# Four heads' maxima first, four heads' exponentials second: regrouping the score runs of an attention slot

## The chip, the cores and the metric

The kernel runs on one core of a Trainium2 chip. The metric is the device time of one execution in microseconds. The core has five instruction streams: TensorE (PE, whose weight loads the profile lists apart as PEld), VectorE (DVE), ScalarE (ACT), GpSimd (POOL) and SyncE (SP, which here only issues DMAs). Each works through its own queue in order, and they wait for each other through semaphores.

## The reference

One transformer layer on x of shape (2, 1024, 512), all in float32: a layer norm, attention with 32 heads of 16 features, a residual, a second layer norm, a quantised gated feed-forward part (512 to 1376 to 512), and a second residual. Cut to what matters here:

```python
q, k, v = (proj(w_q), proj(w_k), proj(w_v))          # (B, 32, S, 16)
scores = jnp.einsum('bhqd,bhkd->bhqk', q, k) / jnp.sqrt(jnp.float32(D_K))
attn = jax.nn.softmax(scores, axis=-1)
out = jnp.einsum('bhqk,bhkd->bhqd', attn, v)
x = x + out.transpose(0, 2, 1, 3).reshape(B, S, HIDDEN) @ w_o.T
x = x + ffn(layernorm(x))      # int4 inputs, ternary weights, relu squared, int8 middle
```

With 2 batches, 32 heads and 1024 by 1024 scores, the attention scores are by far the largest thing computed, and they are computed twice: once for the maximum of each row of scores, once for the exponentials.

## The kernel before, in words

**Steps and slots.** The attention is cut into 32 steps (`steps`): 2 batches, 2 blocks of 512 queries, 4 groups of eight heads, 2 halves of a group. A step thus holds four heads, 512 queries and all 1024 keys. Each step has eight slots (`NT`) of work of two kinds:

- A maximum slot takes four heads and 128 queries by 512 keys (`max_mm`, line 590). Queries stand on the PSUM partitions, so VectorE reduces along the row (`max_reduce`, line 600). After eight such slots all row maxima of the step are there; `max_parts` and `max_rows` turn them into a row `mrow` by four small TensorE transposes into a tile `psn` (line 613).
- An exponential slot takes four heads, 128 keys and 512 queries (`exp_mm`, line 630). Keys stand on the partitions. Three matmuls add up: two for the product of k with the two parts (high and low) of q, and one that adds minus the maximum (`mrow` with `onesr`). ScalarE takes the exponential (`exponentials`, line 634).

Then `weigh_values` (line 660) multiplies the exponentials with v, four heads side by side in the columns of the array, and adds up over the eight slots of the step in one PSUM bank (`pso`).

**Row groups.** A head with its two parts takes 32 rows of TensorE's array of 128, so the four heads of a step lie on four row groups, r = 0 to 3. A tile of scores holds two heads: the pair j = 0 is r = 0 and 1, the pair j = 1 is r = 2 and 3. A tile is 128 partitions by 1024 float32, two PSUM banks. The pool `ps_s` has three such tiles (`bufs=3`), handed out in turn by `scores_psum`, for `psm` (maxima), `pse` (exponentials) and, once in a step, `psn`. Two further banks hold `pso` (pool `ps_a`) and one tile `o` for all filler work (pool `ps_o`).

**The order of work.** The order of instructions is written out by hand: each engine executes them in the order in which the Python code issues them. The loop over T (line 1400) is a software pipeline: slot T issues the maxima of slot T (step `nm`, place `im`), the exponentials of slot T - 10 (`LE`; step `ne`, place `ie`) and the product with v of slot T - 11 (step `nw`, place `iw`). In each slot there are two runs of scores, and `scores(exps, maxs)` issues one run: it takes the tiles from the pool, issues the matmuls of all its tiles in turns (`l` = 0, 1, 2), then the readers of its tiles, the exponentials ahead of the maxima.

In the mixed slots, which are nearly all, the first run takes the exponentials of the pair 0 and the maxima of the pair 1; then comes the product with v, short filler work, the second run with the exponentials of the pair 1 and the maxima of the pair 0, and then the longer filler work. The opening ten slots have only maxima, the last ten only exponentials; these come as one run of four heads.

**Fillers.** All other work (projections of q, k and v, layer norms, the output projection, the feed-forward part of finished rows, the quantising of weights) is cut into small generators. The class `Fillers` hands them out by a planner: `fill.run` gives out work until an estimated cost is used up, and counts its own runs for gaps; neither looks at measured time. A filler that needs TensorE takes the bank `o`, and in the mixed slots at most one filler gets it in each run of the planner. The end of the last block of queries (`the_end`) is ordered by a list scheduler of its own.

Of the kernel before, what the change touches and what calls it, by code (L numbers as in the profile page):

```python
# [233 lines left out]
def kernel(  # L234
# [101 lines left out]
    def scores_psum(name):  # L336
        return ps_s.tile([P, 2, QB], F32, tag="s", name=name)
# [224 lines left out]
    def places(n):  # L562
        kst[n] = sb.tile([P, S], F32R, tag="kst", name=f"kst_{n}", bufs=3)
        qst[n] = [sb.tile([P, QB], F32R, tag="qst", name=f"qst_{n}_{l}", bufs=6) for l in range(2)]

    def load_k(n, first=0):
        nc.sync.dma_start(kst[n][:, first:].bitcast(F32), step_k(n)[:, :, first:])

    def load_q(n):
        b, h, g, s = steps[n]  # L570
        for l, q in enumerate(qst[n]):
            rows = qD[b, g, h][l].rearrange("(r s e) q -> s r e q", r=4, s=2)[s]
            nc.sync.dma_start(q.bitcast(F32), rows)

    def load_v(n):
        b, h, g, s = steps[n]
        vt[n] = sb.tile([P, NT, 4, 32], F32, tag="v", name=f"v_{n}", bufs=2)
        nc.sync.dma_start(vt[n].rearrange("p t r e -> p (t r e)"), vD[b, g, s].rearrange("p t e -> p (t e)"))

    def max_tile(n, i, j):  # L580

        if i == 0 and n not in pm:
            pm[n] = sp.tile([P, TQ, 2, 4], F32, tag="pm", name=f"pm_{n}")
        return scores_psum(f"psm_{n}_{i}_{j}")

    def max_mm(n, i, j, ps, l):
        kh, t = divmod(i, TQ)
        for r in (2 * j, 2 * j + 1):
            rows = slice(32 * r, 32 * r + 32)
            nc.tensor.matmul(  # L590
                ps[:, r % 2, :],
                qst[n][l][rows, t * P : (t + 1) * P],
                kst[n][rows, kh * QB : (kh + 1) * QB],
                start=(l == 0),
                stop=(l == 1),
            )

    def max_reduce(n, i, j, ps):
        kh, t = divmod(i, TQ)
        nc.vector.tensor_reduce(pm[n][:, t, kh, 2 * j : 2 * j + 2], ps, AX.X, ALU.max, negate=True)  # L600

    def max_parts(n):
        m = sp.tile([P, TQ, 4], F32, tag="m", name=f"m_{n}")
        p = pm.pop(n)
        nc.vector.tensor_tensor(m, p[:, :, 0, :], p[:, :, 1, :], ALU.min)
        cols = mcols[n % 2].rearrange("p t (r c) -> p t r c", r=4)
        nc.vector.tensor_copy(cols[:, :, :, 0], m)
        nc.vector.tensor_tensor(cols[:, :, :, 1], m, cols[:, :, :, 0].bitcast(F32), ALU.subtract)
# [12 lines left out]
    def exp_mm(n, i, j, ps, l):  # L621
        for r in (2 * j, 2 * j + 1):
            rows = slice(32 * r, 32 * r + 32)
            if l < 2:
                left, right = kst[n][rows, i * P : (i + 1) * P], qst[n][l][rows, :]
            else:

                rows = slice(32 * r, 32 * r + 2)
                left, right = onesr[rows, :], mrow[n][rows, :]
            nc.tensor.matmul(ps[:, r % 2, :], left, right, start=(l == 0), stop=(l == 2))  # L630

    def exponentials(n, i, j, ps):
        e = sb.tile([P, 2, QB], F32, tag="e", name=f"e_{n}_{i}_{j}", bufs=4)
        nc.scalar.activation(e, ps, AF.Exp, scale=SCALE)  # L634
        probs.setdefault((n, i), {})[j] = e

    def scores(exps, maxs):


        es = [(*x, scores_psum(f"pse_{x[0]}_{x[1]}_{x[2]}")) for x in exps]  # L640
        ms = [(*x, max_tile(*x)) for x in maxs]
        for l in range(3):
            for x in es:
                exp_mm(*x, l)
            if l or not es:
                for x in ms:
                    max_mm(*x, l - bool(es)) if l - bool(es) < 2 else None
        for x in es:
            exponentials(*x)
        for x in ms:  # L650
            max_reduce(*x)
# [3 lines left out]
    def weigh_values(n, i):  # L655
        if i == 0:
            acc[n] = ps_a.tile([P, QB], F32, tag="a", name=f"pso_{n}")
        e = probs.pop((n, i))
        for r in range(4):
            nc.tensor.matmul(  # L660
                acc[n][32 * r : 32 * r + 32, :],
                vt[n][:, i, r, :],
                e[r // 2][:, r % 2, :],
                start=(i == 0),
                stop=(i == NT - 1),
            )
        if i == NT - 1:
            po[n] = sb.tile([P, QB], F32, tag="po", name=f"po_{n}", bufs=3)
            nc.scalar.copy(po[n], acc[n])

    def normalise(n):


        b, h, g, _ = steps[n]
        p0, p1 = po.pop(n - 1), po.pop(n)
        dD = dram.tile([4, 2, QB], F32, name=f"dD_{n}")
        rD = dram.tile([4, 2, QB], F32, name=f"rD_{n}")
        yield ("gap", 3)
        for s, p in enumerate((p0, p1)):
            nc.sync.dma_start(dD[:, s, :], p[16 * (1 - s) :: 32, :])  # L680
        yield ("gap", 4)
        k = 8 * QB // P
        den = sp.tile([P, k], F32, tag="den", name=f"den_{n}", bufs=2)
        nc.sync.dma_start(den, bass.AP(dD.tensor, dD.offset, [[k, P], [1, k]]))
        yield ("gap", 6)
        for c in (slice(0, QB // 2), slice(QB // 2, QB)):
            nc.vector.copy_predicated(p0[:, c], second.to_broadcast([P, QB // 2]), p1[:, c])
            yield ("gap", 1)
        nc.vector.reciprocal(den, den)
        yield ("gap", 2)  # L690
        nc.sync.dma_start(bass.AP(rD.tensor, rD.offset, [[k, P], [1, k]]), den)
        yield ("gap", 3)
        rden = sb.tile([P, QB], F32, tag="rden", name=f"rden_{n}", bufs=1)
        nc.sync.dma_start(
            rden, bass.AP(rD.tensor, rD.offset, [[QB, 8], [0, 16], [1, QB]])
        )
        yield ("gap", 4)
        OT[b, h, g] = sb.tile([P, QB], F32, tag="OT", name=f"OT_{b}_{h}_{g}", bufs=5)
        nc.gpsimd.tensor_tensor(OT[b, h, g], p0, rden, ALU.mult)  # L699
# [617 lines left out]
    def load_slot(n):  # L1317

        return NT * n - (4 if n == 2 else 5)
# [5 lines left out]
    def due_v(n):  # L1325
        return NT * n + (8 if n < 8 else 5)
# [64 lines left out]
    def feed():  # L1391

        while ffns and set(ffns[0][2]) <= fill.done | {ffns[0][2][0]}:
            name, gen, after, due, cost, by = ffns.popleft()
            fill.add(name, gen, after, "ffn", due, cost, by)
# [4 lines left out]
    for T in range(LE + NT * NSTEP + 1):  # L1400
        fill.slot = T
        ne, ie = divmod(T - LE, NT)
        nm, im = divmod(T, NT)
        nw, iw = divmod(T - LE - 1, NT)

        fill.scores = int(T < LE - 1 or T >= NT * NSTEP)

        n = T // NT + 1
        if 1 < n < NSTEP and T == load_slot(n):
            b, h, g, s = steps[n]  # L1410
            fill.ensure(f"k_{b}_{g}_0", f"k_{b}_{g}_1", f"q_{b}_{g}_{h}")
            places(n)
            load_k(n)
            load_q(n)
        n = (T - 5) // NT
        if 0 <= n < NSTEP and T == due_v(n):
            b, h, g, s = steps[n]
            fill.ensure(f"v_{b}_{g}_0", f"v_{b}_{g}_1")
            load_v(n)
        if im == 0 and 0 < nm <= NSTEP:  # L1420
            max_parts(nm - 1)
        exps = [(ne, ie, j) for j in range(2)] if 0 <= ne < NSTEP else []
        maxs = [(nm, im, j) for j in (1, 0)] if nm < NSTEP else []
        mixed = bool(exps and maxs)
        if mixed:
            scores(exps[:1], maxs[:1])
        elif exps:
            scores(exps, [])
        if 0 <= nw < NSTEP:
            weigh_values(nw, iw)  # L1430
            if iw == NT - 1 and nw % 2 and nw < NSTEP - 1:
                b, h, g, _ = steps[nw]
                fill.add(f"norm_{b}_{h}_{g}", normalise(nw), (), "back")
            if iw == NT - 1 and nw == NSTEP - 2:
                fill.add("tokens", first_tokens(nw), (), "ffn", 0)
        feed()
        fill.run(100.0, short=True)
        if mixed:
            scores(exps[1:], maxs[1:])
        elif maxs:  # L1440
            scores([], maxs)
        if im == 1 and 0 < nm <= NSTEP:
            max_rows(nm - 1)
        share = min(max(fill.pace([w[4:] for w in ffns]), SHARE), MORE)
        left = fill.run(share + min(left, SHARE))
# [52 lines left out]
```

## Time and profile before

| | |
|---|---|
| time, median of 3 runs | 1178.94 us (1177.97 to 1180.83) |
| profiled execution, span | 1179.7 us |
| TensorE matmuls busy | 1154.8 us, 98% |
| VectorE busy | 868.8 us, 74% |
| ScalarE busy | 686.8 us, 58% |
| GpSimd busy | 264.1 us, 22% |
| granted TensorE clock, mean | 0.999 |
| row maxima (line 600) | 512 of 1222 ns |
| exponentials (line 634) | 512 of 1023 ns |

The span is that of one profiled execution, from its first to its last instruction; it lies within the range of the timed runs. Busy time counts an engine as busy while any of its instructions is running. TensorE's matmuls overlap each other, in different row or column groups of the array and in the pipeline, so their durations can't be added up. The timeline lists instructions in order of time: start, duration, engine, line, operation, what is written and what is read, shapes, how many were merged into one line (x8), and in brackets how long the engine had been idle before and what ended that. For TensorE the starts of the weight loads tell best when a block of work begins.

### The profile page before, as it was taken

The numbers are of one execution on the slowest core, as the hardware profiler recorded it, in microseconds if no ns is written. First come the engines' busy times: TensorE is split into PE (matmuls) and PEld (weight loads), VectorE is DVE, ScalarE is ACT, GpSimd is POOL, SyncE is SP. The second block draws the span as 40 slices with busy tenths as digits, with TensorE's granted clock in tenths as the row PEclk, the third lists the DMA queues.
The fourth block names the chain that finished last, engine by engine and source line by source line (L and its number), as shares of the span: only waits on it lengthen the run. The fifth ranks groups of instructions, "written<-read, shape, count | busy, mean of one in ns | idle before, by whom it ended". The sixth has DMA issues, their size and how long they took to land.

```text
span 1179.7 us, 21990 instructions
## 1 busy us (share of the span) xinstructions
PE 1154.8 (98%) x8922; PEld 522.5 (44%) x8922; DVE 868.8 (74%) x1261; ACT 686.8 (58%) x878; POOL 264.1 (22%) x319
## 2 busy tenths in 40 slices
PE   8899999999999999999999999999999999999998
PEld 5454444544444444544444445444444433444344
DVE  6765577898876677788866665786988788888467
ACT  2058765556565556566665555465666555665746
POOL 3224336465501101221011011022110001220111
PEclk9999999999999999999999999999999999999999
DMA  5666765556623323443633324244442516362300
GB/s 157 174 183 194 249 197 176 172 190 197 194 93 96 103 55 110 113 95 77 94 86 121 124 59 147 84 130 138 84 97 60 89 53 83 58 81 55 79 9 37
DMA packets 97099, 135.35 MB, mean 115 GB/s; under 512 B 34829, under 2 KB 54285, under 8 KB 96997
## 3 DMA queue, kind: packets, MB, share of 16 engines
q1 hardware_dynamic: 87204, 105.75, 34.6%
q0 software_dynamic: 9792, 28.19, 7.7%
q8 instruction: 70, 1.15, 0.4%
q14 instruction: 33, 0.26, 0.1%
HBM read 89.25 MB, written 37.19 MB: 107 GB/s over the span
## 4 chain that ended last, share of the span: by engine, by line
PE 81%; DVE 5%; DMA 5%; issue 2%; POOL 2%; SPq 2%; ACT 2%; POOLq 0%; DVEq 0%; ACTq 0%
PE pse L630 25%; PE pso L660 18%; PE psm L590 9%; PE psv L533 4%; PE psk L476 4%; PE psy L847 4%; PE psq L476 4%; PE pu L937 2%; PE py L1006 2%; DVE pm L600 2%; PE pg L937 2%; DMA rden<-rD 1%; PE psn L613 1%; SPq L505 1%; PE end L1161 1%
## 5 line engine op out<-in xcount | busy, mean ns | idle before, releaser
L600 DVE TENSOR_REDUCE pm<-psm 128x2 f32<-128x1024 f32 x512 | 623.8, 1222 | 242.9 <-PE pse L630 146.0
L634 ACT ACTIVATE e<-pse 128x1024 f32<-128x1024 f32 x512 | 522.7, 1023 | 408.2 <-PE pse L630 307.3
L590 PE MATMUL psm<-kst,qst 32*128 32x512 f32 x2048 | 369.5, 444 | 7.3 <-DMA kst<-kD 3.8
L630 PE MATMUL pse<-qst,kst 32*128 32x512 f32 x2048 | 367.6, 442 | 3.9 <-DVE pm L600 3.1
L630 PEld LDWEIGHTS pse<-qst,kst 32*128 32x128 f32 x2048 | 149.2, 183 | 332.8 <-issue 199.7
L660 PE MATMUL pso<-e,v 128*32 128x512 f32 x2048 | 272.9, 605 | 0.0
L630 PE MATMUL pse<-mrow,onesr 2*128 2x512 f32 x1024 | 203.9, 396 | 0.0
L590 PEld LDWEIGHTS psm<-kst,qst 32*128 32x128 f32 x2048 | 151.3, 183 | 25.5 <-ACT e L634 10.8
L630 PEld LDWEIGHTS pse<-mrow,onesr 2*128 2x128 f32 x1024 | 94.5, 183 | 3.3
L951 POOL TENSOR_TENSOR g<-g 128x460 f32<-128x460 f32 (+1 forms) x36 | 34.7, 964 | 244.7 <-ACT g L947 237.4
L660 PEld LDWEIGHTS pso<-e,v 128*32 128x32 f32 x2048 | 40.4, 108 | 94.4 <-issue 93.7
L807 POOL TENSOR_SCALAR low<-raws,whalf 128x512 bf16<-128x512 f32 (+2 forms) x35 | 52.0, 1488 | 30.5 <-DMA raws<-in_wuT 8.1
L476 PE MATMUL psq<-xnT,wq 128*128 128x512 f32 x112 | 57.8, 626 | 0.0
L533 PE MATMUL psv<-wv,xnT 128*128 128x128 f32 x384 | 53.2, 285 | 0.0
L533 PEld LDWEIGHTS psv<-wv,xnT 128*128 128x128 f32 x384 | 45.9, 191 | 12.5 <-issue 11.7
L847 PE MATMUL psy<-wo,OT 128*128 128x512 f32 x96 | 49.6, 625 | 0.0
L476 PE MATMUL psk<-xnT,wk 128*128 128x512 f32 x96 | 49.5, 624 | 0.0
L699 POOL TENSOR_TENSOR OT<-po,rden 128x512 f32<-128x512 f32 x15 | 19.2, 1278 | 99.5 <-PE pse L630 52.8
L547 POOL DMA_DIRECT2D vD<-vst x30 | 16.7, 559 | 110.5 <-ACT vst L545 107.8
L909 POOL TENSOR_SCALAR xn<-x,mv,a 128x512 f32<-128x512 f32 x12 | 25.1, 2089 | 71.5 <-DVE a L885 71.5
L937 PEld LDWEIGHTS <-xqT 128*128 128x128 bf16 x288 | 22.4, 98 | 37.8 <-issue 23.8
L937 PE MATMUL pg<-wg,xqT 128*128 128x460 fp8e4 (+1 forms) x144 | 34.2, 360 | 0.0
(227 smaller groups left out, 945.1 us busy)
## 6 DMA issues: line engine op xcount, KB each, us to landing
v<-vD SPq DMA_DIRECT2D x32, 512.0 KB
kst<-kD SPq DMA_DIRECT2D x31, 512.0 KB
qst<-qD SPq DMA_DIRECT2D x60, 256.0 KB
vD<-vst POOLq DMA_DIRECT2D x30, 256.0 KB, 5.7
qD<-hi_q SPq DMA_DIRECT2D x28, 256.0 KB
qD<-lo_q SPq DMA_DIRECT2D x28, 256.0 KB
x<-in_x SPq DMA_DIRECT2D x20, 256.0 KB
rden<-rD SPq DMA_DIRECT2D x15, 256.0 KB
```

The lines of the kernel that those rows point to most:

```text
L476: nc.tensor.matmul(ps, w[:, c, :], xnT[b, h][:, c, :], start=(c == 0), stop=(c == KC - 1))
L533: nc.tensor.matmul(ps[:, i * P : (i + 1) * P], xnT[b, half][:, c, i * P : (i + 1) * P], w[:, c, :], start=(c == 0), stop=(c == KC - 1),)
L590: nc.tensor.matmul(ps[:, r % 2, :], qst[n][l][rows, t * P : (t + 1) * P], kst[n][rows, kh * QB : (kh + 1) * QB], start=(l == 0), stop=(l = ...
L600: nc.vector.tensor_reduce(pm[n][:, t, kh, 2 * j : 2 * j + 2], ps, AX.X, ALU.max, negate=True)
L630: nc.tensor.matmul(ps[:, r % 2, :], left, right, start=(l == 0), stop=(l == 2))
L634: nc.scalar.activation(e, ps, AF.Exp, scale=SCALE)
L660: nc.tensor.matmul(acc[n][32 * r : 32 * r + 32, :], vt[n][:, i, r, :], e[r // 2][:, r % 2, :], start=(i == 0), stop=(i == NT - 1),)
L807: nc.gpsimd.tensor_scalar(low, w, h[:rows, m, 1:2], None, ALU.is_lt)
L847: nc.tensor.matmul(ps, OT[b, h, g][:, i * P : (i + 1) * P], wo[g], start=(g == 0), stop=(g == NG - 1),)
L909: nc.gpsimd.tensor_scalar(xn, xt, mean, a, ALU.subtract, ALU.mult)
L937: nc.tensor.matmul(ps, xT[:, c, :], w[:, c, n : n + size], start=(c == 0), stop=(c == KC - 1))
L951: nc.gpsimd.tensor_tensor(g2[j], g2[j], g2[j], ALU.mult)
```

## The change

A mixed slot's first run becomes the maxima of both pairs, and its second run, behind the product with v, the exponentials of both pairs. In the slots with maxima only, the run moves from the second place to the first; in the slots with exponentials only, from the first to the second. Nothing else is changed: the same matmuls, readers and fillers are issued, and the pool keeps its three tiles.

```diff
         exps = [(ne, ie, j) for j in range(2)] if 0 <= ne < NSTEP else []
         maxs = [(nm, im, j) for j in (1, 0)] if nm < NSTEP else []
-        mixed = bool(exps and maxs)
-        if mixed:
-            scores(exps[:1], maxs[:1])
-        elif exps:
-            scores(exps, [])
+        if maxs:
+            scores([], maxs)
         if 0 <= nw < NSTEP:
             weigh_values(nw, iw)
...
         feed()
         fill.run(100.0, short=True)
-        if mixed:
-            scores(exps[1:], maxs[1:])
-        elif maxs:
-            scores([], maxs)
+        if exps:
+            scores(exps, [])
         if im == 1 and 0 < nm <= NSTEP:
             max_rows(nm - 1)
```

## The prediction

> **What bounds the kernel now.** I read the page first, for the bound and the chain:
>
> ```profile
> span 1179.7 us, 21990 instructions
> PE 1154.8 (98%) x8922; PEld 522.5 (44%) x8922; DVE 868.8 (74%) x1261; ACT 686.8 (58%) x878; POOL 264.1 (22%) x319
> ...
> PE 81%; DVE 5%; DMA 5%; issue 2%; POOL 2%; SPq 2%; ACT 2%; POOLq 0%; DVEq 0%; ACTq 0%
> ...
> L600 DVE TENSOR_REDUCE pm<-psm 128x2 f32<-128x1024 f32 x512 | 623.8, 1222 | 242.9 <-PE pse L630 146.0
> L634 ACT ACTIVATE e<-pse 128x1024 f32<-128x1024 f32 x512 | 522.7, 1023 | 408.2 <-PE pse L630 307.3
> ```
>
> TensorE is the bound, but a busy PE here can be four small matmuls side by side or two, so its 98% says nothing of how well the time is used. The two PSUM readers that the change touches are next: 1222 ns for each row maximum on VectorE, 1023 ns for each exponential on ScalarE. So I went on to the timeline of one slot in the middle, where the weight loads (PEld) mark where each block of TensorE work begins:
>
> ```profile
> 503.84 1.07 PE L660 MATMUL pso<-e,v 128*32 128x512 f32 x8
> 504.84 0.29 PEld L630 LDWEIGHTS pse<-qst,kst 32*128 32x128 f32 x4 [0.84 <-issue]
> 505.74 0.50 PEld L937 LDWEIGHTS <-xqT 128*128 128x128 bf16 x4 [0.37 <-issue]
> 505.89 1.23 DVE L600 TENSOR_REDUCE pm<-psm 128x2 f32<-128x1024 f32 x1 [0.71 <-PE pse L630]
> 505.91 1.02 ACT L634 ACTIVATE e<-pse 128x1024 f32<-128x1024 f32 x1 [0.99 <-PE pse L630]
> 506.62 0.29 PEld L630 LDWEIGHTS pse<-qst,kst 32*128 32x128 f32 x4 [0.38 <-issue]
> 507.64 0.16 PEld L660 LDWEIGHTS pso<-e,v 128*32 128x32 f32 x8 [0.36 <-issue]
> ```
>
> From product with v to product with v: product 1.00, second run 0.90, filler 0.88, next first run 1.02, together 3.80 us. Each run hands one tile to ScalarE and one to VectorE, and they start together, 0.15 to 0.17 us after the next block's loads.
>
> I took the same four numbers from the timeline for the 244 mixed slots from 67.7 to 1089 us (1021.4 us of the span), F being the filler's share. Four kinds appear: 74 slots with F under 1.0 (mean period 3.81), 86 with F near 1.07 (3.90), 54 with F from 1.36 up (mean F 2.14, period 4.99), and 30 that also hold psn, the row of maxima (mean F 1.58, period 4.48). All follow one rule: 2.81 + F, but never under 3.80. The floor shows in a slot with no filler at all:
>
> ```profile
> 813.98 1.02 ACT L634 ACTIVATE e<-pse 128x1024 f32<-128x1024 f32 x1 [0.88 <-PE pse L630]
> ...
> 815.05 0.18 PEld L590 LDWEIGHTS psm<-kst,qst 32*128 32x128 f32 x2 [1.14 <-ACT e L634]
> ```
>
> The maximum matmuls of the next run need the PSUM tile that this exponential is reading; they go 0.05 us after it ends. So a slot is already held by ScalarE when its filler is short.
>
> **The change: what TensorE itself saves.** No instruction is added or removed, and each engine gets its fillers, and SP and POOL their DMAs, in the same order as before; only the score matmuls and their readers move. Both new forms of run are in the trace: the opening slots are all maxima, the last ones all exponentials.
>
> ```profile
> 43.27 0.30 PEld L590 LDWEIGHTS psm<-kst,qst 32*128 32x128 f32 x8 [0.76 <-DVE pm L600]
> 43.94 0.30 PEld L476 LDWEIGHTS psk<-xnT,wk_first 128*128 128x128 f32 x2 [0.36 <-issue]
> 44.04 2.36 DVE L600 TENSOR_REDUCE pm<-psm 128x2 f32<-128x1024 f32 x2 [0.41 <-PE psm L590]
> ```
>
> ```profile
> 1101.86 0.30 PEld L630 LDWEIGHTS pse<-qst,kst 32*128 32x128 f32 x8 [0.38 <-issue]
> 1102.77 0.16 PEld L660 LDWEIGHTS pso<-e,v 128*32 128x32 f32 x8 [0.37 <-ACT po L669]
> 1102.93 1.94 ACT L634 ACTIVATE e<-pse 128x1024 f32<-128x1024 f32 x2 [0.35 <-PE pse L630]
> ```
>
> Eight maxima take 0.67 us, twelve exponential matmuls 0.91, together 1.58 against 0.905 + 0.905 = 1.81 now. In the mixed run the exponentials need three turns of their two row groups and the maxima only two, so two row groups stand idle for one turn in each run; that is 0.23 us a slot.
>
> The Trainium skill has the same mechanism ("TensorE: Matmul & The Clock Gate", Why this matters for your kernels): four matmuls in distinct row groups run at once, 3.07 times as fast for K=32, N=512. By that rule alone the sum would be the gain worked out as the second rival below.
>
> **What the change adds: two waits.** The pool of score tiles has three buffers, so every tile waits for the reader of the third tile before it. The order was e0 m1 e1 m0 (e exponentials, m maxima, the figure the head pair); it becomes m1 m0 e0 e1. Now e1 waits for the reduce of m1 of its own slot, and the next slot's m0 waits for e0. And both exponentials end later after the second run, while the next product needs both. I count from the second run's end, t, which is where the next block's loads begin.
>
> First wait, ScalarE. e0 starts at t + 0.16 and the pair takes 1.94, so e1 is done at t + 2.10, and the product goes on at t + 2.15. It sends head rows 0 and 1 earlier, but the matmul that waits for e1 is third in its queue and holds the rest: product, second run and all fillers behind it. Then product 1.00 and second run 0.91: a new floor of 4.06 us instead of 3.80.
>
> Second wait, VectorE. In the all-maxima run the reduce starts 0.77 after the run's first load (43.27 to 44.04) and lasts 1.22; with 0.05 to release, e1 can go 2.04 after that load. The product's end comes 0.67 + 1.00 = 1.67 after it. TensorE stands for the 0.37 between, with the rest of the second run queued behind e1. So with a long filler the slot is F + 2.04 + 0.91 = F + 2.95, against F + 2.81 now: the 0.23 saved is more than eaten.
>
> Below F of 1.2 the second wait is hidden: m0 cannot start before e0 is free (t + 0.16 + 1.02 + 0.05 = 1.23), m1's two turns run ahead of it, its reduce releases e1 at about t + 3.1, and the product ends at t + 3.15 anyhow. That cover is 0.05 us thin; without it these slots lose what VectorE is late.
>
> The sum by kind: F under 1.0: 4.06 - 3.80 = 0.26, x74 = 19.2. F near 1.07: 4.06 - 3.88 = 0.18, x86 = 15.5. Longer F: 0.14 x54 = 7.6. Slots with psn: psn takes a tile in the rotation, so m1 then waits for e0 and m0 for e1 (t + 2.15, past the mean F of 1.58); m1's second turn starts there, its reduce at about 2.6, e1 goes at 3.87, the period is 4.78 against 4.39: 0.39 x30 = 11.7. Together 54 us.
>
> The last ten slots have no maxima. Now exponentials, product of the slot before, filler; then product first, directly after filler. The wait of 2.15 is covered by the filler alone: gaps of 0.88, 0.88, 0.59, 0, 0, 1.91 and 1.06 leave about 1.27, 1.27, 1.56, 1.92, 2.14, 0.24 and 1.09 uncovered (two of these slots lose 0.2 already): 9.5 us. The opening slots only move their maxima ahead of the short fillers: nothing, since kst and the fillers arrive in the same order; if a kst landing came in between, the cost is the 1 us or so between the two places, once or twice.
>
> Queue lateness is the term that the trace does not show for the new order. VectorE starts the first run's reduce 0.32 us after it could on average (0.15 is usual, one in five is late by 0.2 or more); ScalarE's start at the second run averages 0.18 against 0.10. From below: the readers of both tiles now come in one block and leave VectorE about 1.7 us in one piece for filler work, where it had two gaps of about 0.6, and stalls that exist now (7.7 us over all slots) may vanish under the new floor: -8. From above: 0.17 in each of the 242 slots: +41. I take +5, nearer the lower end, as the pair's readers are out of each other's way and most slots have the floor.
>
> The skill speaks against the change too ("TensorEngine Tiling (Array Packing)", PSUM Bottleneck): tiling speeds TensorE but not the emptying of PSUM, which should use both ScalarE and VectorE. The rows above agree in direction: 1.94 and 2.36 for the pair on one engine, against 1.02 beside 1.23. The page has no price, so its sum would stay the one from the rows.
>
> Sum: 54.0 + 9.5 + 5 = 68.5 on the profiled 1179.7, that is 1248.2. The profiled span is 0.8 above the median of the runs, 1178.94, so I say 1247.
>
> **The rivals.**
> 1. Only ScalarE's wait counts (the reduce of m1 releases earlier than I think, or psn slots hide theirs): 19.2 + 15.5 + 9.5 = 44, about 1223. For it: short-filler slots are 160 of 244. Against it: 0.77 and 1.22 are both read from rows. Chance 0.10.
> 2. Faster: the waits are covered and TensorE's saving shows: F + 2.58 with the old floor of 3.80, so -7 in the slots near 1.07, -0.23 x84 = -19 in the long ones, 1153. It decides if e1 can start within 1.67 us of the maxima's first load and the product within F + 0.67 of the second run's end. The row at 815.05, where a matmul stood for exactly such a tile, speaks against. Chance 0.03.
> 3. Queue lateness at its upper end, VectorE late in each slot as it is now: 1179.7 + 63.5 + 41, about 1284. For it: VectorE is 74% busy and has the longer pair. Chance 0.09.
> 4. The two cancel and nothing is seen: 0.01.
>
> **How the numbers follow.** My case has 0.77; its own range is 1232 to 1262 (psn slots at 0 or at 0.77, lateness -8 to +12). With half of rivals 1 and 3 the range for 8 in 10 is 1224 to 1275. A difference under 0.3% (3.5 us) cannot be told from none here. Faster 0.03, same 0.01, slower 0.96.
>
> **What would show it.** In the profile after: all-maxima runs of 0.67 and exponential runs of 0.91; PEld pse waiting for DVE pm about 0.4 us in slots with long fillers, PEld pso waiting for ACT e in those with short ones; FFN slots (F 0.88) at 4.06 instead of 3.80; TensorE's busy share lower, with the counts unchanged. I am wrong if the second run starts 1.00 after the product without a wait, if slots with short fillers stay at 3.80, or if the two waits stand but add up to under 30 us.

## The result, and the profile after

The changed kernel takes 1275.15 us (median of 4 runs, 1273.04 to 1277.04) against 1178.83 for the kernel before on the same chip: ratio 1.0809, 95% interval 1.0791 to 1.0827. It is slower, as forecast, and by 28 us more than forecast. All differences in the profile below are between the two profiled executions, 1271.3 and 1179.7 us: 91.6 us.

From the page of the changed kernel: the engines' busy time, and the chain that ended last by engine:

```profile
PE 1220.2 (96%) x8922; PEld 530.8 (42%) x8922; DVE 852.1 (67%) x1261; ACT 660.5 (52%) x878; POOL 264.0 (21%) x319
...
PE 68%; DVE 8%; issue 7%; POOL 6%; DMA 6%; ACT 3%; SPq 2%; POOLq 0%; ACTq 0%; DVEq 0%
```

The work is the same: 8922 matmuls, and by the groups further down the page 512 reduces of 1219 ns and 512 exponentials of 1021 ns. No engine became the bound. TensorE's share of the chain fell from 81% to 68%, and what grew is DVE (5 to 8%), POOL (2 to 6%) and issue (2 to 7%). VectorE and GpSimd have no more to do than before (852.1 us busy after 868.8, 264.0 after 264.1), so they stand in the chain because something waits for them. For GpSimd the forecast had no such wait.

A slot with a short filler, from the timeline (columns: start, duration, engine, line, operation, and in brackets the idle time before and its releaser):

```profile
551.84 0.40 PEld L660 LDWEIGHTS pso<-e,v 128*32 128x32 f32 x8 [0.37 <-issue]
...
553.07 0.30 PEld L630 LDWEIGHTS pse<-qst,kst 32*128 32x128 f32 x8 [0.84 <-issue]
...
553.98 0.50 PEld L937 LDWEIGHTS <-xqT 128*128 128x128 bf16 x4 [0.37 <-issue]
...
554.16 1.94 ACT L634 ACTIVATE e<-pse 128x1024 f32<-128x1024 f32 x2 [1.67 <-PE pse L630]
...
555.23 0.30 PEld L590 LDWEIGHTS psm<-kst,qst 32*128 32x128 f32 x6 [0.18 <-ACT e L634]
...
555.90 0.14 PEld L660 LDWEIGHTS pso<-e,v 128*32 128x32 f32 x4 [0.37 <-issue]
```

From product to product it is 551.84 to 555.90, the 4.06 us of the forecast. The exponentials start 0.18 after the second run's end (553.98) and end at 556.10; m0 goes 0.05 after the first of them (555.23). The next product waits for the end of the pair. Its first four loads go at 555.90; the other four, from the timeline just behind:

```profile
556.15 0.14 PEld L660 LDWEIGHTS pso<-e,v 128*32 128x32 f32 x4
```

They go 0.05 after the exponentials' end. That is why a product in such a slot takes 1.23 (551.84 to 553.07) instead of 1.00.

A slot with a longer filler and with psn, from the same timeline:

```profile
710.96 0.16 PEld L660 LDWEIGHTS pso<-e,v 128*32 128x32 f32 x8 [0.36 <-issue]
...
711.08 2.36 DVE L600 TENSOR_REDUCE pm<-psm 128x2 f32<-128x1024 f32 x2 [2.59 <-PE psm L590]
711.96 0.18 PEld L630 LDWEIGHTS pse<-qst,kst 32*128 32x128 f32 x2 [0.84 <-PE psm L590]
...
712.35 0.29 PEld L630 LDWEIGHTS pse<-qst,kst 32*128 32x128 f32 x6 [0.21 <-DVE pm L600]
...
713.48 0.52 PEld L613 LDWEIGHTS psn<-identr,mcols 128*128 128x128 f32 x4 [0.60 <-DVE pm L600]
...
715.88 0.16 PEld L660 LDWEIGHTS pso<-e,v 128*32 128x32 f32 x8 [0.37 <-issue]
```

The product is undisturbed (1.00), e0 sends its two matmuls, and e1 stands until the reduce of m1 ends at 712.30: its loads come 0.39 after those of e0. psn then stands again, until the second reduce ends at 713.44. The next maxima begin at 715.02 and take 0.86 instead of 0.67, since m0 waits for e1, whose exponential ends at 715.17. The first and the last of these waits were in the forecast. psn's own wait was not: TensorE's loads stand idle for 0.60 before psn, where 0.37 is usual between two blocks.

So the waits were as described. The surplus is elsewhere, and the view of waits points to it (columns: microseconds in total, times, longest):

```profile
PEld pse L630 <- DVE pm L600: 37.8, 71, 3.8
...
DVE wg L809 <- POOL low L807: 8.3, 4, 2.5
...
DVE xn L911 <- POOL xn L909: 6.3, 5, 2.9
```

A wait of 0.39 for a reduce was foreseen; one of 3.8 was not. VectorE's own waits for GpSimd at line 809 have grown to 21.5 us in 11 places; before they were 5.4 us in 8. One of the eleven, from the timeline around 270 us:

```profile
269.68 1.57 POOL L807 TENSOR_SCALAR low<-raws,whalf 128x512 bf16<-128x512 f32 x1
...
271.29 1.87 DVE L809 SCALAR_TENSOR_TENSOR wu<-raws,whalf,low 128x512 fp8e4<-128x512 f32 x1 [1.39 <-POOL low L807]
...
273.54 2.35 DVE L600 TENSOR_REDUCE pm<-psm 128x2 f32<-128x1024 f32 x2
...
274.80 0.30 PEld L630 LDWEIGHTS pse<-qst,kst 32*128 32x128 f32 x6 [2.96 <-DVE pm L600]
```

VectorE's next instruction needs `low`, which GpSimd finishes at 271.25. Behind it in VectorE's queue stand a layer norm step of 0.53 us (line 391) and then the two reduces. Their matmuls began at 269.73, so by the 0.77 of the prediction they could have started at about 270.5; they start at 273.54, e1 of the same slot waits for the first of them, and TensorE's loads stand for 2.96 us. VectorE's wait is 1.39 of these 3.0 us. The instruction behind the wait also ran long: 1.87 us, where the median of line 809's 35 is 0.74.

The slots counted as in the prediction, from the end of one second run to the next, as F plus a median remainder:

| kind | slots before / after | before | after | change, forecast | change, measured | x slots after |
|---|---|---|---|---|---|---|
| F under 1.0 | 74 / 75 | 2.92 | 3.17 | 0.26 | 0.25 | 18.8 |
| F near 1.07 | 86 / 86 | 2.81 | 2.95 | 0.18 | 0.14 | 12.0 |
| longer F | 54 / 53 | 2.81 | 2.95 | 0.14 | 0.14 | 7.4 |
| with psn | 30 / 30 | 2.81 | 3.03 | 0.39 | 0.22 | 6.6 |

That is 45 us, where 54 were forecast. The 244 mixed slots as a whole grew by 80.8 us (1021.4 to 1102.2), so 36 us lie above the medians. They are in few places: measured from product to product, 19 slots lie more than 0.5 us above the median of their kind, by 32.8 us together; before there were 4 such slots with 3.6. Of the 32.8 us, 22.4 lie in nine slots in which VectorE waits for GpSimd at line 809 or 911, 2.7 in four slots right behind such a wait, 4.8 in two slots behind a wait of ScalarE for a DMA at 148 us, and 2.9 in four others. The last ten slots grew by 9.6 (35.1 to 44.7; forecast 9.5), the opening and the end by 1.2.

### The profile page after: what moved, and what is told of

It is laid out like the page before. It is cut to its first block, busy times and chain, and to the rows that moved or that the text cites. A ratio compares the mean times of both kernels' runs of the same rounds, so it can differ in the third digit from the quotient of the medians.

```text
span 1271.3 us, 22010 instructions
## 1 busy us (share of the span) xinstructions
PE 1220.2 (96%) x8922; PEld 530.8 (42%) x8922; DVE 852.1 (67%) x1261; ACT 660.5 (52%) x878; POOL 264.0 (21%) x319
## 4 chain that ended last, share of the span: by engine, by line
PE 68%; DVE 8%; issue 7%; POOL 6%; DMA 6%; ACT 3%; SPq 2%; POOLq 0%; ACTq 0%; DVEq 0%
PE pso L660 16%; PE pse L630 15%; PE psm L590 12%; DVE pm L600 6%; PE psv L533 4%; PE psy L847 3%; PE psk L476 3%; POOL low L807 3%; PE psq L476 3%; PE py L1006 3%; PE pu L937 2%; PE pg L937 2%; ACT e L634 2%; DMA rden<-rD 1%; PE psn L613 1%
## 5 line engine op out<-in xcount | busy, mean ns | idle before, releaser
L600 DVE TENSOR_REDUCE pm<-psm 128x2 f32<-128x1024 f32 x512 | 602.8, 1219 | 275.7 <-PE psm L590 273.0
L634 ACT ACTIVATE e<-pse 128x1024 f32<-128x1024 f32 x512 | 496.4, 1021 | 494.1 <-PE pse L630 494.1
L660 PE MATMUL pso<-e,v 128*32 128x512 f32 x2048 | 318.6, 612 | 3.7 <-ACT e L634 3.5
L630 PE MATMUL pse<-qst,kst 32*128 32x512 f32 x2048 | 238.4, 453 | 21.2 <-DVE pm L600 21.0
L590 PE MATMUL psm<-kst,qst 32*128 32x512 f32 x2048 | 227.8, 456 | 10.2 <-ACT e L634 5.8
L630 PEld LDWEIGHTS pse<-qst,kst 32*128 32x128 f32 x2048 | 108.4, 184 | 255.8 <-issue 161.2
L590 PEld LDWEIGHTS psm<-kst,qst 32*128 32x128 f32 x2048 | 98.7, 185 | 153.0 <-issue 71.0
L630 PE MATMUL pse<-mrow,onesr 2*128 2x512 f32 x1024 | 138.8, 394 | 0.0
L660 PEld LDWEIGHTS pso<-e,v 128*32 128x32 f32 x2048 | 62.2, 108 | 120.8 <-issue 90.9
L960 DVE TENSOR_TENSOR inter<-pu,g 128x460 f32<-128x460 f32 (+1 forms) x36 | 22.9, 635 | 30.0 <-PE pu L937 29.1
L669 ACT COPY po<-pso 128x512 f32<-128x512 f32 x32 | 18.8, 587 | 37.7 <-PE pso L660 28.6
L937 PEld LDWEIGHTS <-xqT 128*128 128x128 bf16 x288 | 22.4, 98 | 37.0 <-issue 23.0
```

The costliest lines, as they stand in the source:

```text
L590: nc.tensor.matmul(ps[:, r % 2, :], qst[n][l][rows, t * P : (t + 1) * P], kst[n][rows, kh * QB : (kh + 1) * QB], start=(l == 0), stop=(l = ...
L660: nc.tensor.matmul(acc[n][32 * r : 32 * r + 32, :], vt[n][:, i, r, :], e[r // 2][:, r % 2, :], start=(i == 0), stop=(i == NT - 1),)
L937: nc.tensor.matmul(ps, xT[:, c, :], w[:, c, n : n + size], start=(c == 0), stop=(c == KC - 1))
```

## The experiments

My theory at this point: two waits as forecast, and a lateness of VectorE that only became expensive because e1 now needs the reduce of its own slot. The rivals: only one of the waits counts; the loss lies in the grouping itself; the lateness comes from elsewhere (the clock, the weights' DMAs).

**The last ten slots (tail_first).** The changed kernel, but in the slots without maxima the exponentials go first again.

```diff
         if maxs:
             scores([], maxs)
+        elif exps:
+            scores(exps, [])
...
-        if exps:
+        if exps and maxs:
             scores(exps, [])
```

> The changed kernel, but the last ten slots, which have only exponentials, issue them in the first place again, ahead of the product of the slot before. Theory (the product waits for a pair of exponentials that now stand right in front of it): the product's weight loads no longer wait about 0.9 us on ScalarE in those slots, and the 9.6 us that the stretch from the last mixed slot to the last product grew by come back: about 1265.5 us against 1275. Rival (that stretch is set by the fillers and the final block, which only start later for another reason): 1275, no change.

1263.62 us (1254.21 to 1270.65), ratio 1.0705 (1.063 to 1.078). The last ten slots take 35.3 us, as before the change (35.1), 9.4 less than in the changed kernel. That term of the forecast stands. The runs of this kernel differ by 16 us from each other, so the profile's slots say it more sharply than the median.

**The reduce shortened (half_reduce).** The reduce reads half of the scores of its tile, so half of the maximum is left out, here and in the two later kernels that contain this edit. Everything else is as in the changed kernel.

```diff
-        nc.vector.tensor_reduce(pm[n][:, t, kh, 2 * j : 2 * j + 2], ps, AX.X, ALU.max, negate=True)
+        nc.vector.tensor_reduce(pm[n][:, t, kh, 2 * j : 2 * j + 2], ps[:, :, : QB // 2], AX.X, ALU.max, negate=True)
```

> The changed kernel, but each row maximum on VectorE reads only the first half of its keys (128 x 2 x 256 instead of 128 x 2 x 512), so half of the maximum is left out; matmuls, tiles and waits stay. A reduce should fall from 1.22 to about 0.69 us, so e1 can go about 1.5 us after the maxima's first load, before the product's end at 1.67. Theory (second wait, VectorE, sets the long slots and its queue's lateness is the term that was too small): slots with long fillers fall from F + 2.95 to F + 2.58, 53 x 0.37 = 20 us; slots with psn lose some 0.3 x 30 = 9; the late starts of the reduce cost less, some 10; short slots stay at 4.06, held by ScalarE: about 1237 us (1228 to 1256). Rival (ScalarE's pair in front of the product is the whole loss): 1275, no change.

1245.09 us (1241.18 to 1247.4), ratio 1.0538 (1.0504 to 1.0571). From the page:

```profile
L600 DVE TENSOR_REDUCE pm<-psm 128x2 f32<-128x512 f32 x512 | 329.4, 685 | 443.0 <-PE psm L590 440.8
```

The wait for the reduce is gone from the slots with long fillers (F + 2.57 instead of F + 2.95, so all that TensorE saves shows there), and the floor stays where ScalarE puts it: 4.05. VectorE does 273 us less work, and the kernel is still 5% slower than before.

**The product one slot later (late_product).** The product with v takes the exponentials of two slots ago instead of one, so it never meets an exponential that is still running.

```diff
-    for T in range(LE + NT * NSTEP + 1):
+    for T in range(LE + NT * NSTEP + 2):
...
-        nw, iw = divmod(T - LE - 1, NT)
+        nw, iw = divmod(T - LE - 2, NT)
```

> The changed kernel, but the product with v of a slot is issued one slot later (slot T - 12 instead of T - 11; one more slot at the end), so that it never waits for the exponentials issued just before it; tiles, runs and readers stay. Theory (two waits, each near 4.06 in short slots: m0 waits for e0 until 1.23, its pair's reduce then frees e1 at about 3.1): short slots fall only from 4.06 to about 4.01, 160 x 0.05 = 8 us; long ones stay; the last ten slots get back about 9 and pay about 2 for the slot added: about 1260 us. Rival (the product's wait alone holds the short slots): they fall to the old floor of about 3.8, 160 x 0.25 = 40, and with the tail about 1227.

1255.19 us (1250.88 to 1258.4), ratio 1.0624 (1.0586 to 1.0662). Slots with F under 1.0 come back to 3.84, those with F near 1.07 stay at 4.03, and those with long fillers keep F + 2.95. The time is near the theory's 1260, but for the short slots the theory was wrong: it had 4.01 there, the rival 3.8. From the timeline, in such a slot:

```profile
563.61 1.94 ACT L634 ACTIVATE e<-pse 128x1024 f32<-128x1024 f32 x2 [1.44 <-PE pse L630]
563.65 0.50 PEld L937 LDWEIGHTS <-xqT 128*128 128x128 bf16 x4 [0.37 <-issue]
564.53 0.45 PEld L590 LDWEIGHTS psm<-kst,qst 32*128 32x128 f32 x8 [0.38 <-issue]
```

Here e1 stands for the reduce while e0 goes on, so the exponentials start 0.04 before the second run's end (563.65), not 0.16 after it, and m0 gets its tile earlier. What is left is the second wait alone, F + 2.95. This is the mirror image of the kernel above: each edit takes away one wait and leaves the other.

**Both (late_half).** The two edits together.

> Both of the last two edits: the product one slot later and the row maxima over half of the keys (half of the maximum left out). Theory (the two waits cover each other in short slots, and TensorE's own saving of 0.23 us a slot is real under them): short slots max(F, 1.23) + 2.58, about 3.81, 160 x 0.25 = 40 us; long slots F + 2.58, 53 x 0.37 = 20; psn slots and lateness some 20; tail 7: about 1188 us (1172 to 1202), near or just above the kernel before. Rival (the regrouped runs save TensorE nothing when they stand among the others): long slots no better than F + 2.81 and short ones about 4.0, about 1225.

1204.59 us (1199.27 to 1208.51), ratio 1.0195 (1.0156 to 1.0234): 17 us above the expectation. One edit gave 30 us, the other 20, both 71. The 21 us beyond the sum come mainly from the slots with F near 1.07: they stayed at 4.04 and 4.03 with either edit alone and fall to 3.80 with both, so there each wait covers for the other. A slot with a short filler, from its timeline:

```profile
562.15 0.16 PEld L660 LDWEIGHTS pso<-e,v 128*32 128x32 f32 x8 [0.36 <-issue]
...
565.29 0.29 PEld L590 LDWEIGHTS psm<-kst,qst 32*128 32x128 f32 x6 [0.18 <-ACT e L634]
...
565.95 0.16 PEld L660 LDWEIGHTS pso<-e,v 128*32 128x32 f32 x8 [0.36 <-issue]
```

The period is 3.80. The product takes 1.00 (the next block begins at 563.15), the second run 0.90 (to 564.05), and the floor is the one of before, m0 waiting for e0 (565.29). Long slots are at F + 2.57 too, where the second rival of the prediction had 2.58. So without the two waits the medians of the slots without psn are where the model puts them, and yet the kernel is slower than before. The slots with psn stay long (4.72, against 4.31 before the change). The rest is lateness: 21 slots are late by 33.0 us. The expectation missed because I had taken it to go with the waits.

**GpSimd's results asked for later (gap_after), and the control (gap_before).** A filler that hands work from GpSimd to VectorE yields in between, for a number of runs of the planner. Both such places get two runs more, in the changed kernel and in the kernel before:

```diff
             nc.gpsimd.tensor_scalar(low, w, h[:rows, m, 1:2], None, ALU.is_lt)
-            yield ("gap", 1)
+            yield ("gap", 3)
...
             nc.gpsimd.tensor_scalar(xn, xt, mean, a, ALU.subtract, ALU.mult)
-            yield ("gap", 2)
+            yield ("gap", 4)
```

> The changed kernel, but VectorE's instructions that use a result of GpSimd (the quantised weight from the mask low, and the clipping of xn) are issued two planner runs, that is one slot, later after GpSimd's own, so that VectorE finds the result ready and does not stand in front of the row maxima. Theory (the term that was too small is VectorE standing in its queue for GpSimd, with m1's reduce behind it and e1 behind that): the stalls of the slots near 195, 257, 270, 306, 331, 349, 636 and 1132 us, some 20 us together with their after-effects, go: about 1255 us against 1275. Rival (VectorE is late from its own load, or the stalls come from DMAs): 1275, no change.

> The same two delays in the kernel before, as a control. Theory (there the reader of a tile has a whole run of slack, so VectorE's standing for GpSimd is hidden): 1179 us, no change beyond 4 us. Rival (the delays help any order of the runs): about 20 us faster, 1160.

In the changed kernel: 1245.81 us (1244.54 to 1249.46), ratio 1.0543 (1.0492 to 1.0595), 29 us less. In the kernel before: 1182.35 us (1180.91 to 1187.05), ratio 1.0015 (0.9995 to 1.0035), no difference. VectorE's waits for GpSimd at line 809 in gap_after, all that is left of 21.5 us:

```profile
DVE wd L809 <- POOL low L807: 0.2, 1, 0.2
```

The medians are those of the changed kernel (4.04 and 4.02; F + 2.95; with psn 4.49 after 4.48), so the two waits are untouched; the late slots hold 5.0 us instead of 32.8. This shows that most of the surplus over the forecast comes from VectorE standing for GpSimd, and that the same two-run delay is worth nothing in the old order. It does not separate the waits from line 809's long runs: in the changed kernel three took over 1.8 us, here the longest takes 1.05.

**Waits and lateness removed (late_half_gap).** late_half with the longer gaps.

> The changed kernel with all three edits: the product one slot later, the row maxima over half of the keys (half of the maximum left out), and VectorE's uses of GpSimd results one slot later. Theory (two waits that cover each other, plus VectorE standing for GpSimd and what follows from it; nothing else): the 29 us that the last edit gave to the changed kernel come off 1204.6 nearly whole: about 1177 us (1170 to 1184), level with the kernel before, though its tail is 1 us and its psn slots 10 us longer: TensorE's saving then shows. Rival (the edits take away the same stalls, the shorter reduce already having removed the lateness): about 1200.

1175.32 us (1172.6 to 1179.31) against 1181.16, ratio 0.9952 (0.9935 to 0.997). The mixed slots take 1009.6 us, against 1021.4 before and 1018.4 in gap_before: with both waits and the lateness away, the idle row groups that the change fills show up as a gain at last. It is less than the 26 us of the prediction's second rival, since slots with psn stay long (4.72 against 4.31). No run halves the reduce in the kernel before; but in its long slots product and runs alone (1.00 + 0.905 + 0.905) make up the 2.81, so a shorter reduce has nothing to gain there. late_half_gap needs half of the reduce left out, so it is no version of this kernel.

**Another way to raise the floor (swap_product).** The kernel before, with the product behind the second run and the long filler between the runs, in the mixed slots:

```diff
+        if mixed:
+            share = min(max(fill.pace([w[4:] for w in ffns]), SHARE), MORE)
+            feed()
+            left = fill.run(share + min(left, SHARE))
+            scores(exps[1:], maxs[1:])
+        elif maxs:
+            scores([], maxs)
+        if im == 1 and 0 < nm <= NSTEP:
+            max_rows(nm - 1)
         if 0 <= nw < NSTEP:
             weigh_values(nw, iw)
...
         if mixed:
-            scores(exps[1:], maxs[1:])
-        elif maxs:
-            scores([], maxs)
-        if im == 1 and 0 < nm <= NSTEP:
-            max_rows(nm - 1)
+            continue
```

> The kernel before (two and two heads in each run), but the product with v and the longer filler change places: first run, long filler, second run, product, short filler. All three tiles then have a longer stretch between reader and next use in short slots: m1 needs e1 at 1.23 after the second run and comes 1.00 + 0.33 after it. Theory (the old floor of 3.80 is e1 of the second run holding m1 of the next first run): FFN slots fall from 3.80 to about 3.71, 74 x 0.09 = 7 us, others stay at F + 2.81: about 1172 us. Rival (a new wait in place of it, m0 for e0 across a short filler, or late VectorE work): 1180 or slower.

1191.63 us (1185.36 to 1193.69), ratio 1.0082 (1.0056 to 1.0109): a miss, with the wrong sign, and by the wait that the rival names. From its timeline, a slot with a short filler:

```profile
1031.20 0.30 PEld L630 LDWEIGHTS pse<-qst,kst 32*128 32x128 f32 x4 [0.84 <-issue]
1031.32 0.30 PEld L590 LDWEIGHTS psm<-kst,qst 32*128 32x128 f32 x4
...
1032.97 0.30 PEld L630 LDWEIGHTS pse<-qst,kst 32*128 32x128 f32 x4 [0.38 <-issue]
1033.34 0.18 PEld L590 LDWEIGHTS psm<-kst,qst 32*128 32x128 f32 x2
```

In a mixed run the maxima start 0.12 after the exponentials (1031.20, 1031.32), not a turn later as I had assumed. In the second run they come 0.37 behind (1032.97, 1033.34), because m0 needs the tile of e0, whose exponential follows the first run across a filler of 0.88 only (1032.09 to 1032.97). So the same wait for ScalarE moved to the other side of the product, the slots stay at 3.80, and the slots with psn got longer (median 4.46 from product to product, against 4.32 before), about 7 us in all. Where the rest of the 11.5 us lies stays open.

**The other grouping (reverse_gap).** gap_after with the exponentials of both pairs in the first run and the maxima of both pairs in the second.

```diff
-        if maxs:
-            scores([], maxs)
+        if exps:
+            scores(exps, [])
...
-        if exps:
-            scores(exps, [])
+        if maxs:
+            scores([], maxs)
```

> The same regrouping the other way round: the first run has all four heads' exponentials, the second, behind the product, all four heads' maxima (with VectorE's uses of GpSimd results one slot later, as in the run before that had this edit alone on the changed kernel, 1245.8 us). The product then never waits, m0 waits for e0 until 1.23 after the first run, and the next e1 waits for m1's reduce until about 1.15 after the second. Theory (the recurrences of the three tiles decide, with the numbers of the prediction): slots F + 2.81 from F of 1.15 up and 3.96 below, so 74 x 0.16 = 12 and 86 x 0.08 = 7 us, psn slots 0.9 x 30 = 27 because e1 waits there for m0's reduce, the last ten slots as before: about 1228 us (1212 to 1240). Rival (four heads of one kind in a run are what costs, in either order): 1246 as in the other order.

1209.95 us (1208.91 to 1212.28), ratio 1.0249 (1.0222 to 1.0276): below the expected range, and 36 us better than gap_after with the same runs the other way round. So four heads of one kind in a run are not in themselves what costs. From its timeline:

```profile
554.45 2.35 DVE L600 TENSOR_REDUCE pm<-psm 128x2 f32<-128x1024 f32 x2 [1.59 <-PE psm L590]
...
555.73 0.30 PEld L630 LDWEIGHTS pse<-qst,kst 32*128 32x128 f32 x6 [0.29 <-DVE pm L600]
...
556.62 0.16 PEld L660 LDWEIGHTS pso<-e,v 128*32 128x32 f32 x8 [0.37 <-issue]
```

The floor is as expected, 3.95 (here 3.94, from a product at 552.68 to the next at 556.62): 0.99 of product, 0.78 to the reduce, 1.22 of reduce, 0.06 to e1's loads, 0.89 of run. Long slots are at F + 2.81, also as expected, since a long filler covers the reduces. What missed are the slots with psn. I expected them near 5.3, and their median is 4.32 (F + 2.81). One of them, further on in the same timeline:

```profile
744.25 2.35 DVE L600 TENSOR_REDUCE pm<-psm 128x2 f32<-128x1024 f32 x2 [3.23 <-PE psm L590]
744.60 0.52 PEld L613 LDWEIGHTS psn<-identr,mcols 128*128 128x128 f32 x4 [0.62 <-ACT e L634]
...
746.14 0.30 PEld L630 LDWEIGHTS pse<-qst,kst 32*128 32x128 f32 x8
```

I had e1 wait for the second reduce, which ends at 746.60. All eight loads of the first turns go at 746.14. The pool does not hand out its tiles strictly in turn here: in this kernel as built, e1 gets back the tile of psn, not that of m0, in all 31 places. psn's reader is a copy of 0.59 us on ScalarE that starts at 745.30, so e1 is free of the second reduce.

## Why the forecast was right in sign and short in size

**TensorE's saving.** Right. All-maxima runs take 0.67 where nothing waits, all-exponential runs 0.90 to 0.91, and late_half shows the 2.57 that follows for a slot.

**First wait, ScalarE.** Right: floor 4.06 forecast, 4.04 to 4.05 measured; late_product takes it to 3.84.

**Second wait, VectorE.** Right: F + 2.95 forecast and measured; half_reduce removes it. Rival 1 (only ScalarE's wait counts) falls with that. In the short slots it is better hidden than forecast: alone it gives 3.84 (late_product), not the 4.01 that a cover of 0.05 would mean.

**Slots near 1.07, and slots with psn.** Both forecast too high: 0.14 for 0.18, and 0.22 for 0.39. The former stay just under the forecast floor: F + 2.95 is 4.02 for an F of 1.07, and 4.03 is the median. In the latter the order of the waits is as forecast, but not their time: I had the exponentials start 0.16 after the second run's end and free m0 at t + 2.15. In the slot at 710.96 they start 0.25 before the next block (713.23 against 713.48), since e1 and psn had stood before it, and m0 is free at 715.22, t + 1.74. The reduce follows 0.57 later. All kinds together are 9 us less than forecast.

**The last ten slots.** 9.6 for 9.5, confirmed by tail_first.

**Queue lateness: the step that failed.** The prediction put +5 here, "nearer the lower end, as the pair's readers are out of each other's way". It measured about 36 (80.8 less 45), and gap_after makes the kernel 29 us faster. My bounds were made by a delay in every slot: 0.17 for 242 slots. It is not like that: most slots have the median, and 19 hold nearly all. The missing thought is the slack of the reduces. Before, a reduce of the second run ended at 507.12 (505.89 + 1.23) and its tile was needed by e1 of the next slot's second run, at 508.64 (504.84 + 3.80): 1.5 us of slack, which hid VectorE's waits for GpSimd. After, the first reduce of the pair starts at 551.74 and ends 1.22 later, at 552.96, and e1 wants to go at 553.07: 0.1 of slack; in slots with longer fillers the slack is below zero. I priced the new wait at VectorE's usual speed and did not ask what stands ahead of the reduce in its queue: line 809 and line 911, which wait for GpSimd. (The Trainium skill, "TensorE: Matmul & The Clock Gate", Architectural detail, calls the queues of ScalarE and VectorE strictly first in, first out; the reduces at 273.54, standing behind the wait at 271.29, agree.) The rows for that were in the trace of before: line 809's waits of 5.4 us in 8 places. Rival 3, VectorE late in each slot, comes near the total (1284) by another mechanism, which would have shown in the medians. My own case ended at 1262; that the range for 8 in 10 reached 1275 came from half of rival 3, so that the measured 1275.15 lies at its very edge is luck. Rivals 2 and 4 needed waits that are covered or cancelled; the waits are there.

Not all of the surplus is this wait. At 148 us a ScalarE instruction at line 768 waits 4.73 us for a DMA of raw weights, with the exponentials behind it; gap_after still has a shorter one of 2.84 there. How much of the 36 us is the clock (last section) was not measured by itself.

## What to carry to other kernels

When a change lets one tile wait for a reader of its own slot, price not the reader's duration but the slack that the reader had before, and list what can stand ahead of it in its engine's queue, above all instructions that wait for a third engine. Where two waits end at about the same time, both must be removed before either shows (30 and 20 us apart, 71 together). Judge the order of a pair by which reader has time behind it: exponentials first and maxima second cost 2.5%, the reverse 5.4%, with the same instructions, both with GpSimd's results asked for later.

## What the hardware showed that was not expected

A stall of TensorE cost more than its own length, because the clock fell behind it. The longest wait, with what VectorE did before it and what follows it, from the timeline of the changed kernel:

```profile
1134.00 1.23 DVE L911 TENSOR_SCALAR xn<-xn 128x512 f32<-128x512 f32 x1 [2.90 <-POOL xn L909]
...
1135.66 2.35 DVE L600 TENSOR_REDUCE pm<-psm 128x2 f32<-128x1024 f32 x2
...
1136.93 0.50 PEld L630 LDWEIGHTS pse<-qst,kst 32*128 32x128 f32 x6 [3.79 <-DVE pm L600]
...
1138.51 4.87 PE L1006 MATMUL py<-wd,iqT 128*128 128x512 fp8e4 x11
```

The window behind that wait (columns: the window, its microseconds, busy time and instructions of PE, PEld, DVE, ACT and POOL, the granted clock, DMA share, GB/s):

```profile
1137.00:1143.30 6.30, 6.30 (x21) 2.22 (x21) 1.83 (x3) 2.69 (x3) 0.00 (x0) 0.50 0.10 21
```

In the window ahead of it, 1131.70 to 1137.00, the clock was 0.99. At 0.50 the eleven matmuls of line 1006 take 4.87 us, where they took 2.55 before the change; this slot took 12.41 us. By the clock in the trace, time at half clock was 34.1 us in the changed kernel, 13.7 in gap_after, 3.4 before the change. So up to 15 us, half of the 30.7 more, is an estimate of what the clock added to the stalls; counted the same way, up to 10 of the 29 us that gap_after gives back are the clock.

The Trainium skill ("TensorE: Matmul & The Clock Gate", Part 1 and HAM oscillation) has the rule that gaps of over about 3.4 us without TensorE work bring the clock to half, decided in windows of that length that run freely. The halves here come in pieces of 3.4 and 6.8 us, which agrees. The threshold does not: the profile's idle time before line 630's matmuls was 1.68, 1.90, 2.56 and 2.64 us at four stalls with a fall of the clock within 2 us (after 334, 309, 353 and 274), and 2.17 at one without (after 199).
